# Expert attention: when a block's statistics and factors are computed

## The chip, the cores and the metric

The kernel runs on one core of a Trainium2 chip. A core has five engines that run side by side, each through its own list of instructions in order: TensorE (PE: matmuls, with weight loads shown as PEld), VectorE (DVE), ScalarE (ACT), GpSimd (POOL) and SyncE (SP, which issues most DMAs). An instruction that needs another engine's result waits for a semaphore, and everything behind it on its engine waits too. The metric is the device time of one execution in microseconds (us), lower is better. The kernel before takes 2578.53 us, the median of three runs.

## The reference

A small vision tower is computed: 128 images are cut into 64 tokens of 256 features by two convolutions, then come an attention with a ReLU in place of a product, an attention with experts, a linear attention and a feed-forward layer with experts. The change lies in the third, the expert attention:

```python
def _L0_ffn_ref(x, norm_w, router_w, router_b, qkv_w, proj_w, proj_b, out_w):
    residual = x
    mean = jnp.mean(x, axis=-1, keepdims=True)
    var = jnp.mean((x - mean) ** 2, axis=-1, keepdims=True)
    xn = (x - mean) / jnp.sqrt(var + EPS) * norm_w
    gate = jax.nn.softmax(xn @ router_w.T + router_b, axis=-1)
    ...
    attn = jnp.einsum('bcehtd,bcehsd->bcehts', q, k) * scale
    attn = jax.nn.softmax(attn, axis=-1)
    y = jnp.einsum('bcehts,bcehsd->bcehtd', attn, v)
    ...
    out = jnp.einsum('btceo,bte->btco', y, gate).reshape(B, T, D)
    return residual + out @ out_w.T
...
h = h + _L0_ffn_ref(_layernorm(h, axis=-1), L0_ffn_norm_w, ...)
```

Each token is normalised twice in a row: ahead of this layer (`_layernorm`), where the result is also the layer's residual, and inside it. Both follow from the mean and the variance of the token's 256 features, by a few factors for each token: `rs` and `mr` for the stream (`h` plus its normalised form), `ra` for the layer's input.

## The kernel before

The stream lies in SBUF as `h2`, 128 partitions x 64 pairs x 256 features: a pair is two images, whose 2 x 64 tokens fill the partitions. The expert attention goes through the pairs in the loop of `rest` (L1349), one pair in each turn. In a turn it computes the scores of the current pair (L1116), takes their maxima and subtracts them on VectorE (L1126, L1130), exponentiates on ScalarE (L1133), sums on VectorE (L1136, L1137), and multiplies by the gate and the reciprocal on GpSimd (L1143, L1144). The weights of the pair before are transposed on TensorE (L1152), copied by ScalarE (L1157) and multiplied with the values (`mixed`, L1167); the pair before that gets its output product (L1183) and is added to the stream by VectorE (`added`, L1187). For the next pair, queries and keys (L1034) and values (L1057) are computed; VectorE and ScalarE copy the values out of PSUM (L1071, L1073) and GpSimd adds a bias (L1077).

Nearly all of these PSUM tiles (queries, values, transposes, outputs) come from one ring of four buffers (`sh.psq`), so a product waits until the tile four places earlier has been emptied.

Four pairs make a block. What a block needs ahead of its pairs is spread over earlier turns by a table: `at(n, place, f, ...)` files a step under a turn and a place, and the loop calls `do((p, place))` at nine places. The places that matter here are "POOL", after GpSimd's second weights and before the values, and "DVE", at the end of the turn. The steps of a block b, whose first pair is n = 4b:

- `statistics(n0)` (L863) on VectorE, for two tiles: L870 (`bn_stats`) and L871 (`bn_aggr`), the second of which writes the tile `mv` with mean and variance. Two calls make a block. For b > 2 they are filed in turns n - 11 and n - 10.
- `factors(parts)` (L882) on GpSimd, nine small instructions over 128 x 4 elements. Part 0 is L887 and L888 (a power), part 1 L891 to L893, part 2 L895 (a power) and L896, part 3 L898 and L899. For b > 2 parts 0 and 1 are filed in turn n - 9, parts 2 and 3 in turn n - 8.
- `normal(k)` (L911) on GpSimd, one tile in each of the turns n - 8 to n - 5: L915 computes the normalised tile and reads `mv` and `ra`, then `stream` (L923) updates the stream with `rs` and `mr`.
- transposes, gate logits and the gate itself in turns n - 4 to n - 1.

For the blocks from 3 on, `mv` comes from a ring of two buffers, as `rs` and `mr` do:

```python
elif n0 == 0:
    self.mv = sh.np_.tile([P, 8, 2], F32, tag="mv", name="mv")
```

The order of the instructions on each engine is the order in which the program issues them (`manual_schedule`). Steps filed under the same turn and place run in the order in which they were filed, a lower block's first.

Of the kernel before, what the change touches and what calls it, by code (L numbers as in the profile page):

```python
# [761 lines left out]
def expert_attention(c, sh, front, hd, normw, wr, br, wqkv, wvT, wproj, bproj, wout):  # L762
# [446 lines left out]
    def at(n, place, f, *a):  # L1209
        key = (n, place) if n >= 0 else "first"  # L1210
        work.setdefault(key, []).append(lambda: f(*a))

    for b, x in enumerate(blocks):
        n = NB * b
        if b > 2:
            at(n - 11, "DVE", x.statistics, 0)
            at(n - 10, "DVE", x.statistics, 2)
        if b > 1:
            if b == 2:
                at(n - 7, "POOL", x.factors)  # L1220
            else:
                at(n - 9, "POOL", x.factors, (0, 1))
                at(n - 8, "POOL", x.factors, (2, 3))
            for k in range(NB):
                at((1, 2, 2, 3)[k] if b == 2 else n - 8 + k, "POOL", x.normal, k)
        elif b == 1:
            for k in range(NB):
                at(1 + k // 2, "ACT2", x.stream_scalar, k)
        if b:
            for fc in range(2):  # L1230
                at(n - 4 + fc, "PE", x.transpose, fc)
                at(n - 4 + fc, "ACT", x.transposed, fc)
            at(n - 2, "PE", x.logits_in_strips)
            at(n - 2, "ACT", x.logits_copied)
            at(n - 1, "PE", x.logits_transposed)
            at(n - 1, "DVE0", x.logits_less_max)
            at(n - 1, "ACT1", x.exponents)
            at(n - 1, "DVE1", x.sums)
            at(n - 1, "POOL0", x.gates)
# [18 lines left out]
    x, y, z = blocks[:3]  # L1258
# [1056 lines left out]
@with_exitstack  # L2315
def vit_tower(ctx: ExitStack, tc: tile.TileContext, a, out):
    const = ctx.enter_context(tc.tile_pool(name="const", bufs=1))
    dram = ctx.enter_context(tc.tile_pool(name="dram", bufs=1, space=DRAM))
    c = Ctx(tc, const)

    hd = dram.tile([B, T, D], F32, name="hd")

    hx = dram.tile([B, T, D], F32, name="hx")
    gfd = dram.tile([B * T, 1], F32, name="gfd")
    with tc.tile_pool(name="stream", bufs=1) as sp:
        c.h2 = sp.tile([P, B // 2, D], F32, name="h2")
        tokenizer(c, a["x"], a["w1"], a["bn1"], a["w2"], a["bn2"])
        front = Front(c, hd, *(a[k] for k in ("wqk1", "bqk1", "wv1", "bv1", "wg")))
        with ExitStack() as rings:
            sh = Shared(c, rings, ExitStack())  # L2330
            beside, rest = expert_attention(
                c, sh, front, hd, *(a[k] for k in ("normw", "wr", "br", "wqkvf", "wvf", "wproj", "bproj", "wout"))
            )
            rest(*relu_attention(c, sh, a["wqkv0"], a["wmlp"], a["bmlp"], beside))
    c.tables(ctx.enter_context(tc.tile_pool(name="tables", bufs=1)))
    with tc.tile_pool(name="gate", bufs=1) as gp:
        k = Routing(c, gp, a["wg"], a["bg"])
        with front.ctx:
            linear_attention(c, front, hd, hx, out, k)
        experts(c, hx, gfd, out, a["we1"], a["we2"], a["be2"], lambda: route(c, k, gfd))  # L2340
# [71 lines left out]
```

## Time and profile before

| what | value |
|---|---|
| median of three runs | 2578.53 us (2573.55 to 2582.93) |
| profiled execution | 2578.67 us |
| its span in the profile | 2577.0 us |
| granted TensorE clock, mean | 0.987 |
| tokenizer and the ReLU attention, then the first turn of the pairs | 0 to 1101 us |
| loop over pairs, from pair 1 (1101 to 1780 us) | PE 665.1, DVE 604.9, ACT 495.4, POOL 526.8 us busy of 679 |
| linear attention and experts (1780 to 2577 us) | PE 732.2, DVE 440.5, ACT 288.9, POOL 298.3 us busy of 797 |
| L870, 64 instructions | 407 ns median |
| L871, 64 instructions | 182 ns median |

A row of the page or of an answer is read so: times are microseconds from the start of the span; an instruction is named by its engine, its line in the kernel, its operation and the tiles that it writes and reads (`out<-in`). In a timeline the first number is the start, the second the duration. `[0.16 <-PE sc L1116]` behind a row means that the engine stood idle for 0.16 us before it, and that L1116 on PE ended the wait. In a table of windows the busy time of each engine in each stretch is given, with the number of instructions in brackets.

### The profile page before, as it was taken

The page shows a single profiled execution, that of the slowest core. Times are in us where ns is not written, and L with a number is a line of the kernel's source. Part 1 is how long each engine was busy: PE and PEld are TensorE (multiplying, and loading weights), DVE is VectorE, ACT ScalarE, POOL GpSimd, SP SyncE. Part 2 cuts the span into 40 slices and gives each one's busy share as a digit, 9 for nine tenths or more (in the row PEclk, how much of TensorE's full clock was granted, in tenths as well). Part 3 has the DMA queues.
Part 4 walks back from the last instruction along what each step waited for, and adds up shares of the span by engine and source line. Part 5 has one row for each costly group of instructions (what it writes and reads, how often), then busy time and mean ns, then how long its engine had stood idle before and what let it go on. Part 6 is the DMA issues. An engine that isn't in the chain of part 4 may idle for free. (4 is left out here: it accounts for less than half of the span.)

```text
span 2577.0 us, 78108 instructions
## 1 busy us (share of the span) xinstructions
PE 2463.2 (96%) x33713; PEld 1623.6 (63%) x33713; DVE 2011.8 (78%) x3000; ACT 1631.8 (63%) x3421; POOL 1701.0 (66%) x1491
## 2 busy tenths in 40 slices
PE   7989999999999999899999999999999968999997
PEld 4554444444444444477777777776566547888886
DVE  5759999999999989898898889887667794444443
ACT  2228889898988888776777777775544433323332
POOL 3418989898998999787878787864232404445453
PEclk9999999999999999999999999999999989999998
DMA  3100000000000000000000000001354335555554
GB/s 113 36 13 1 2 2 2 1 2 2 2 2 2 2 2 13 2 28 14 24 14 24 14 24 14 24 14 34 84 121 110 83 89 195 181 192 191 198 190 129
DMA packets 138033, 140.97 MB, mean 55 GB/s; under 512 B 108001, under 2 KB 121859, under 8 KB 129870
## 3 DMA queue, kind: packets, MB, share of 16 engines
q1 hardware_dynamic: 128684, 119.48, 15.5%
q0 software_dynamic: 7648, 14.77, 1.8%
q8 instruction: 267, 4.37, 0.7%
q10 hardware_dynamic: 1344, 1.61, 0.2%
q14 instruction: 90, 0.74, 0.1%
HBM read 104.00 MB, written 32.54 MB: 53 GB/s over the span
## 5 line engine op out<-in xcount | busy, mean ns | idle before, releaser
L540 POOL TENSOR_TENSOR m<-q,k 128x1024 f32<-128x1024 f32 x384 | 719.6, 1908 | 55.8 <-PE sc L342 46.8
L532 DVE TENSOR_TENSOR m<-pc,k 128x2048 f32<-128x2048 f32 (+1 forms) x320 | 646.5, 2056 | 0.5 <-ACT q L472 0.5
L342 PE MATMUL sc<-m,wide 128*32 128x512 f32 x4096 | 520.1, 597 | 8.9 <-ACT m L541 6.6
L541 ACT ACTIVATE m<-m 128x1024 f32<-128x1024 f32 x384 | 402.4, 1049 | 20.5 <-POOL m L540 20.5
L342 PEld LDWEIGHTS sc<-m,wide 128*32 128x32 f32 x4096 | 134.7, 109 | 269.4 <-issue 157.7
L550 ACT ACTIVATE m<-k,q 128x64 f32<-128x64 f32 x1024 | 270.7, 338 | 0.9 <-DVE k L419 0.9
L1144 POOL TENSOR_TENSOR e<-e,mx 128x1024 f32<-128x1024 f32 x127 | 241.6, 1902 | 9.9
L2238 PE MATMUL ph<-xt,w1s 128*128 128x256 f32 x896 | 199.0, 380 | 4.4 <-ACT hT L2242 2.2
L1157 ACT COPY pT<-pt 128x512 f32<-128x512 f32 x256 | 133.4, 597 | 109.5 <-PE pt L1152 109.5
L2254 PE MATMUL po<-w2s,hT 128*128 128x256 f32 x896 | 198.0, 379 | 0.0
L2238 PEld LDWEIGHTS ph<-xt,w1s 128*128 128x128 f32 x896 | 169.8, 190 | 29.2 <-ACT hT L2242 3.4
L2254 PEld LDWEIGHTS po<-w2s,hT 128*128 128x128 f32 x896 | 168.1, 190 | 21.7
L2272 POOL DMA_INDIRECT out<-y,rout x56 | 56.6, 1010 | 168.2 <-ACT hT L2242 129.2
L1126 DVE TENSOR_REDUCE mx<-sc 128x16 f32<-128x1024 f32 x128 | 150.3, 1215 | 21.2 <-PE sc L1116 21.2
L1136 DVE TENSOR_REDUCE mx<-e 128x16 f32<-128x1024 f32 x128 | 154.7, 1209 | 6.6 <-ACT e L1133 4.9
L1133 ACT ACTIVATE e<-e 128x1024 f32<-128x1024 f32 x128 | 133.9, 1060 | 34.3 <-DVE e L1130 30.0
L2242 ACT ACTIVATE hT<-ph,w1s 128x256 f32<-128x256 f32 x224 | 93.0, 470 | 96.9 <-PE ph L2238 82.5
L2259 ACT ACTIVATE y<-y,gf 128x256 f32<-128x256 f32 x56 | 28.0, 507 | 197.3 <-issue 112.3
L1130 DVE TENSOR_TENSOR e<-sc,mx 128x1024 f32<-128x1024 f32 x128 | 150.2, 1214 | 0.1
L1041 ACT COPY kr<-pqk 128x512 f32<-128x512 f32 x248 | 127.3, 601 | 24.2 <-PE pqk L1034 24.2
L1152 PE MATMUL pt<-ident,e 128*128 128x128 f32 x1024 | 130.5, 277 | 11.0 <-POOL e L1144 9.7
L1167 PEld LDWEIGHTS pz<-pT,vr 128*64 128x64 f32 x4096 | 124.7, 138 | 21.1 <-issue 10.6
(346 smaller groups left out, 4856.5 us busy)
## 6 DMA issues: line engine op xcount, KB each, us to landing
w1s<-in_we SPq DMA_DIRECT2D x30, 1028.0 KB
w2s<-in_we SPq DMA_DIRECT2D x30, 1024.0 KB
h<-hd SPq DMA_DIRECT2D x4, 2048.0 KB
hx<-h SPq DMA_DIRECT2D x4, 2048.0 KB
out<-h SPq DMA_DIRECT2D x4, 2048.0 KB
xt<-in_x SPq DMA_DIRECT2D x15, 512.0 KB
hd<-h SPq DMA_DIRECT2D x15, 512.0 KB
x<-hd SPq DMA_DIRECT2D x12, 512.0 KB
```

The costliest lines, as they stand in the source:

```text
L342: nc.tensor.matmul(dst[j : j + 32], wide[:, hf, s : s + 32], part, start=start, stop=stop)
L532: nc.vector.tensor_tensor(m, bcast(self.pq[:, hf, i : i + n], 3, T), k, ALU.max)
L540: nc.gpsimd.tensor_tensor(m, bcast(self.q[:, hf, s : s + 2], 3, T), k, ALU.subtract)
L541: nc.scalar.activation(m, m, AF.Relu)
L550: nc.scalar.activation(self.parts[i, hf][:, q], self.blk.k[:, hf, i], AF.Relu, bias=self.q[:, hf, i - NB // 2, q : q + 1], scale=-1.0,)
L1126: nc.vector.tensor_reduce(mx, self.sc[x].rearrange("p h c s -> p (h c) s"), AX.X, ALU.max)
L1130: nc.vector.tensor_sub(e, self.sc[x].rearrange("p h c s -> p (h c) s"), bcast(self.sm[x], 2, T))
L1133: nc.scalar.activation(self.e[x], self.e[x], AF.Exp, scale=SCALE)
L1136: nc.vector.tensor_reduce(self.sm[x], self.e[x], AX.X, ALU.add)
L1144: eng.tensor_mul(e, e, bcast(sm, 2, T))
L2238: nc.tensor.matmul(ph[:, j], self.w1[:, w0 : w0 + P], self.xt[:, fc], start=(fc == 0), stop=(fc == 1))
L2254: nc.tensor.matmul(po, self.hT[:, f, r * P : r * P + P], self.w2[:, f, :], start=(f == 0), stop=(f == 7))
```

## The change

For the blocks from 4 on, `early` is 2. Their statistics are filed two turns sooner, in turns n - 13 and n - 12. Their factors are filed one part a turn, in turns n - 11, n - 10, n - 9 and n - 8, so that the last part stays where it was and the first moves up by two turns. Blocks 0 to 3 are as before. No instruction is added or removed.

```diff
     for b, x in enumerate(blocks):
         n = NB * b
+        early = 2 * (b > 3)
         if b > 2:
-            at(n - 11, "DVE", x.statistics, 0)
-            at(n - 10, "DVE", x.statistics, 2)
+            at(n - 11 - early, "DVE", x.statistics, 0)
+            at(n - 10 - early, "DVE", x.statistics, 2)
         if b > 1:
             if b == 2:
                 at(n - 7, "POOL", x.factors)
+            elif early:
+                for k in range(4):
+                    at(n - 11 + k, "POOL", x.factors, (k,))
             else:
                 at(n - 9, "POOL", x.factors, (0, 1))
                 at(n - 8, "POOL", x.factors, (2, 3))
```

## The prediction

> **What bounds the kernel now.** I read the page's busy shares first, then the loop over pairs as one window for each pair, then the timeline of one pair boundary, then who waits for whom on single lines.
>
> ```profile
> PE 2463.2 (96%) x33713; PEld 1623.6 (63%) x33713; DVE 2011.8 (78%) x3000; ACT 1631.8 (63%) x3421; POOL 1701.0 (66%) x1491
> ```
>
> TensorE is busiest overall, but a share says nothing about one loop. The changed code runs in the loop over pairs, and that loop repeats every four pairs. A pair is counted here from the start of its scores (L1116): pair 39 starts at 1513.11, pair 43 at 1556.07. The windows below give pairs 39 to 42 and then pairs 56 to 59 (columns: length, then busy us of PE, PEld, DVE, ACT, POOL):
>
> ```profile
> 1513.11:1523.93 10.82, 10.78 (x282) 8.51 (x278) 9.73 (x19) 7.70 (x15) 6.80 (x7) 1.00 0.01 3
> 1523.93:1535.03 11.10, 10.59 (x284) 8.54 (x281) 9.86 (x14) 7.99 (x14) 10.53 (x14) 1.00 0.01 3
> 1535.03:1545.38 10.35, 10.35 (x284) 8.57 (x280) 9.13 (x12) 8.14 (x15) 9.61 (x14) 1.00 0.14 41
> 1545.38:1556.07 10.69, 10.69 (x297) 8.54 (x293) 10.04 (x16) 7.73 (x15) 8.06 (x8) 1.00 0.12 30
> ...
> 1695.62:1706.72 11.10, 10.59 (x284) 8.54 (x281) 9.85 (x14) 7.99 (x14) 9.53 (x10) 1.00 0.02 4
> 1706.72:1717.07 10.35, 10.35 (x285) 8.57 (x281) 9.13 (x12) 8.13 (x15) 4.89 (x6) 1.00 0.14 46
> 1717.07:1727.76 10.69, 10.69 (x297) 8.54 (x293) 9.13 (x12) 7.73 (x15) 5.76 (x6) 1.00 0.09 23
> 1727.76:1738.42 10.66, 10.66 (x282) 8.51 (x279) 8.82 (x15) 7.78 (x15) 4.20 (x5) 1.00 0.01 4
> ```
>
> The second group is a free experiment: no statistics and no factors are left there (and from pair 57 no normalising), and GpSimd is nearly idle. Yet a pair costs the same, and pair 56 the same 11.10 as pair 40, which has factors ahead of it. GpSimd's load does not set the pace. Four pairs cost 42.96 with this work (39 to 42). Without it they cost 11.10 + 10.35 + 10.69 + 10.66 = 42.80, and the gain is in the last one (10.66 for 10.82).
>
> What does set it shows at the boundary from pair 39 to pair 40:
>
> ```profile
> 1522.50 0.36 DVE L1187 TENSOR_TENSOR h<-h,po 128x256 f32<-128x256 f32 x1
> 1522.66 0.21 POOL L1143 TENSOR_TENSOR mx<-mx,gate 128x16 f32<-128x16 f32 x1 [1.11 <-DVE mx L1137]
> 1523.93 1.59 PE L1116 MATMUL sc<-kr 32*64 32x64 f32 x128
> 1524.19 1.22 DVE L1071 TENSOR_TENSOR vr<-pv,xTr 128x512 f32<-128x512 f32 x2
> 1525.57 2.35 DVE L1126 TENSOR_REDUCE mx<-sc 128x16 f32<-128x1024 f32 x2 [0.16 <-PE sc L1116]
> 1526.99 1.23 POOL L915 TENSOR_SCALAR oTr<-h,mv,rs 128x256 f32<-128x256 f32 x1
> 1527.06 1.09 PE L1152 MATMUL pt<-ident,e 128*128 128x128 f32 x8 [0.51 <-POOL e L1144]
> ```
>
> In the pair whose number leaves 3 when divided by four, VectorE is late by the gate's small steps. TensorE waits for it twice: before the second values product (L1057, whose PSUM buffer L1187 empties; the line's own view names L1187 as its releaser 13 times, 6.2 us, once in four pairs) and before the second half of the transposes (L1152, 0.51). So VectorE has little to give from L1126 of one pair to L1187 of the same pair.
>
> **The new wait.** The tile `mv` has two buffers. Statistics of block b write the buffer that block b-2 had, and its last reader is L915, the normalising of that block's fourth tile on GpSimd, in pair 4b-13. Before, statistics began in pair 4b-11, two pairs later, and nothing had to be waited for. Now they begin in pair 4b-13 itself, at the end of VectorE's queue for that pair. The first L871 of each block b = 5 to 15 must wait for that L915: 11 waits. Block 4 moves too, but the last reader of its buffer lies before this loop. Behind L871 stand the next pair's maxima (L1126), for which ScalarE's exponents, GpSimd's weights and then TensorE's transposes wait.
>
> **Its price in one boundary** (block 13, pair 39). L1071 ends at 1524.19 + 1.22 = 1525.41; L870 takes 0.42 more, to 1525.83. L915 ends at 1526.99 + 1.23 = 1528.22. VectorE stands for 2.39. Then the rest of the statistics, read from where they now lie, after pair 41:
>
> ```profile
> 1546.56 0.18 DVE L871 BATCH_NORM_AGGREGATE mv<-st 128x2 f32<-128x6 f32 x1
> 1546.66 0.40 DVE L870 BATCH_NORM_STATS2 st<-h 128x6 f32<-128x256 f32 x1
> 1547.09 0.18 DVE L871 BATCH_NORM_AGGREGATE mv<-st 128x2 f32<-128x6 f32 x1
> 1547.19 1.20 DVE L1126 TENSOR_REDUCE mx<-sc 128x16 f32<-128x1024 f32 x1
> ```
>
> From the first L871 to the maxima is 0.63, so pair 40's maxima start at 1528.85 in place of 1525.57: 3.28 late. How much of that reaches TensorE, step by step:
>
> 1. Pair 41's own chain, which waits for nothing between, takes 6.46 from maxima (1536.66) to the end of L1187 (1542.76 + 0.36). So L1187 of pair 40 ends at 1535.31. Pair 39 shows 1.07 from L1187's end (1522.86) to the next scores (1523.93): scores of pair 41 at 1536.38, not 1535.03. That is 1.35; the other 1.7 was slack.
> 2. GpSimd's weights: 6.26 from maxima to the first L1143 (1542.92 in pair 41) and 4.36 on to the end of the second L1144 (1545.37 + 1.91). For pair 40 that ends at 1539.47. TensorE reaches the second half of the transposes 2.60 after the scores (1.52 and 1.08), at 1538.98, and waits 0.49. TensorE is 1.84 late.
> 3. VectorE ends pair 40 with L1071 (7.79 after the maxima, 1.22 long) and the second half of the statistics (0.99 to the next maxima): pair 41's maxima at 1538.85, 2.19 late. Pair 41's L1187 ended about 1.2 ahead of need, so nothing is added, and no statistics follow it any more: pair 42's maxima are set by the scores again.
> 4. In pair 43 the maxima came 1.82 after the scores, because statistics stood before them; where nothing does it is 1.63 or 1.64. That returns 0.19: VectorE is 1.65 late, and pair 43 is the pair in which it decides.
>
> So four pairs cost 1.65 more. Eleven times: 18.2. After the last block the statistics of pairs 49 and 50 are gone: less 0.2. Sum +18.
>
> **The moved factors.** The nine small steps of a block stay nine. Part 0 (0.20 + 1.03 in the trace, about 1.4 with its gaps) goes behind pair 4b-11, part 1 (three of 0.20, about 0.85) behind 4b-10, part 2 (1.02 + 0.20) behind 4b-9 and part 3 (two of 0.20) ahead of the normalising. I cost them at nothing: GpSimd's idle time ahead of L1143 covers them (2.37 in pair 42, 1.11 and more in pair 43). Taking 2.1 us from behind pair 39 would let pair 40's L1143 start right after its reciprocal, but that now comes about 3 late. Without that cover part 0 would cost at most its 1.4 us. Block 4's statistics go into pair 3 without a wait; by the rows between 0 and 0.9, taken as 0. No DMA is issued by a moved step and SP's order stays.
>
> Bounds for four pairs: at the top the whole 3.28 (11 x 3.28 = 36); at the bottom step 1 alone less step 4, 1.16 (13). A gain is bounded by pairs 56 to 59: 0.16 in four pairs, 2 in all.
>
> The Trainium skill, Perfetto Trace Analysis, section Optimization Strategy, says that the same gap repeating over a stretch can mean that there are too few buffers for the next tile. By that reading the moved statistics make such a gap, a bubble of full size every four pairs, and the sum would be the 36 of the upper bound; the rows above let 1.63 of each 3.28 be absorbed. The same page, section GPSIMD Engine Instruction, distrusts GpSimd's reported spans and advises start-to-start spacing, which for L915 is 1.33 here (1526.99 to 1528.32) instead of 1.23: about 1 us more in all.
>
> **The rivals.**
> - *All of it arrives* (slower still). Later waits of the ring of four PSUM buffers could pass on what step 1 calls slack: 2578.7 + 36 = 2615. Against it: L1187 ends 1.7 ahead of need in pair 40.
> - *VectorE's idle time swallows it* (not slower). It is busy 38.8 of 42.96, so 4.2 is free against a stall of 2.4. It decides if L1187 of pair 40 may come 3.07 later without anyone waiting. The trace speaks against: 1535.03 - 1.07 leaves 1.72. Time 2577 to 2580.
> - *GpSimd's lateness in pair 40 was on the path* (faster). L1143 starts 0.9 after its reciprocal there (1532.85, against 1531.71 + 0.25). If that 0.9 reached TensorE and the new wait did not: 11 x 0.9 = 10, 2569. Pair 56 speaks against it: no factors ahead, and the same 11.10.
> - *The change doesn't act as read*: no wait, because the second buffer is free in time. L915 would have to end before 1525.83; it ends 2.39 later, by two weights of 1.90 that go before it. Then 2577 to 2580, counted with the second rival.
>
> **How the numbers follow.** The profiled execution took 2578.67: its span of 2577.0 and 1.67 around it. The median of the three runs is 2578.53, so both bases agree. Forecast: 2577.0 + 18 + 1.67 = 2597. Chances: forecast 0.80 (its own range, from the bottom of 13 to some 29: 2591 to 2608), all of it 0.12, swallowed or not acting 0.06, faster 0.02. For 8 in 10 the range reaches down for a part of the swallowed case and up to the bound: 2588 to 2614. What a measurement can tell from no change is 0.3%, 7.7 us: slower means above 2586. Slower 0.92, same 0.06, faster 0.02.
>
> **What would show it.** After: VectorE idle before L871, released by GpSimd's L915, 11 times and about 2.4 each, 26 in all; four pairs take 44.6; L1057's wait for L1187 doubles in count; the maxima of the pair after each wait come some 5 after their scores instead of 1.64; times from pair 52 on shift only. The prediction is wrong if L871 has no GpSimd wait, if the four pairs stay at 43.0, or if the pairs without a wait grow too.

## The result

The changed kernel takes 2600.59 us (median of six runs, 2599.38 to 2605.42), the kernel before in the same comparison 2578.32 (2573.55 to 2583.15). The ratio is 1.0088 with a 95% interval from 1.0071 to 1.0104: slower by 0.9%, some 22 us. The prediction said 2597, with a range from 2588 to 2614.

The profiled execution after has a span of 2597.7, 20.7 more than before. Its busy times hardly differ from before, which is the first thing to read in it: no engine got more work.

```profile
PE 2471.4 (95%) x33713; PEld 1625.6 (63%) x33713; DVE 2008.5 (77%) x3000; ACT 1632.6 (63%) x3421; POOL 1701.6 (66%) x1491
```

The same four pairs as before, 39 to 42, as one window each (length, then busy us of PE, PEld, DVE, ACT, POOL):

```profile
1528.46:1539.12 10.66, 10.66 (x282) 8.51 (x279) 8.82 (x15) 7.78 (x15) 7.22 (x10) 1.00 0.01 3
1539.12:1551.58 12.46, 11.01 (x284) 8.66 (x281) 9.80 (x16) 7.21 (x13) 9.06 (x10) 1.00 0.01 3
1551.58:1562.65 11.07, 10.85 (x283) 8.70 (x281) 10.73 (x18) 8.92 (x16) 9.32 (x11) 1.00 0.13 38
1562.65:1573.34 10.69, 10.69 (x297) 8.54 (x293) 9.13 (x12) 7.73 (x15) 9.46 (x10) 1.00 0.13 31
```

The pair after the wait went from 11.10 to 12.46, the next from 10.35 to 11.07, the pair of the wait itself from 10.82 to 10.66. Four pairs take 44.88 in place of 42.96: 1.92 more. The eleven blocks with the wait make 11 x 1.92 = 21.1. From the scores of pair 4 to those of pair 63 the trace has 658.40 against 636.85, 21.55 more, so the loop holds all of the loss. The pairs from 52 on, behind the last wait, have their old lengths.

VectorE at the boundary from pair 39 to pair 40, with GpSimd's L915, in the timeline after:

```profile
1540.51 0.42 DVE L870 BATCH_NORM_STATS2 st<-h 128x6 f32<-128x256 f32 x1
...
1542.17 1.23 POOL L915 TENSOR_SCALAR oTr<-h,mv,rs 128x256 f32<-128x256 f32 x1
...
1543.44 0.18 DVE L871 BATCH_NORM_AGGREGATE mv<-st 128x2 f32<-128x6 f32 x1 [2.51 <-POOL oTr L915]
...
1544.07 2.32 DVE L1126 TENSOR_REDUCE mx<-sc 128x16 f32<-128x1024 f32 x2
...
1546.31 2.35 DVE L1130 TENSOR_TENSOR e<-sc,mx 128x1024 f32<-128x1024 f32 x2
...
1547.58 2.22 PE L1034 MATMUL pqk<-xTr 64*64 64x256 f32 x32 [0.91 <-DVE e L1130]
```

L870 was done at 1540.93. L871 stood for 2.51 until L915 was done with `mv`, and the maxima came 4.95 after their scores (1539.12), where before it was 1.64. The last row is the one that the prediction did not have: TensorE's queries and keys (L1034) now wait for VectorE's L1130. L1034's own view, taken from 1190 us on, shows it in ten of the eleven waits (microseconds in total, times; one row of PE and two of PEld for each wait, so the sum counts some time twice). In the kernel before, the same view lists no wait at all:

```profile
  DVE e L1130: 24.3, 30
```

L871's own view over the whole span names L915 eleven times, by the three tiles that it writes in turn; before, it lists no wait:

```profile
  POOL xTr L915: 10.1, 4
  POOL xnr L915: 10.1, 4
  POOL oTr L915: 7.5, 3
```

### The profile page after: what moved, and what is told of

It reads as the page before. It is cut to its first block, busy times and chain, and to the rows that moved or that the text cites. A ratio compares the mean times of both kernels' runs of the same rounds, so it can differ in the third digit from the quotient of the medians.

```text
span 2597.7 us, 78064 instructions
## 1 busy us (share of the span) xinstructions
PE 2471.4 (95%) x33713; PEld 1625.6 (63%) x33713; DVE 2008.5 (77%) x3000; ACT 1632.6 (63%) x3421; POOL 1701.6 (66%) x1491
## 5 line engine op out<-in xcount | busy, mean ns | idle before, releaser
L1144 POOL TENSOR_TENSOR e<-e,mx 128x1024 f32<-128x1024 f32 x127 | 241.6, 1902 | 9.9
L1130 DVE TENSOR_TENSOR e<-sc,mx 128x1024 f32<-128x1024 f32 x128 | 150.1, 1213 | 0.1
L1152 PE MATMUL pt<-ident,e 128*128 128x128 f32 x1024 | 132.4, 278 | 11.2 <-POOL e L1144 8.9
L1041 ACT COPY kr<-pqk 128x512 f32<-128x512 f32 x248 | 127.3, 601 | 17.4 <-PE pqk L1034 17.3
L1167 PEld LDWEIGHTS pz<-pT,vr 128*64 128x64 f32 x4096 | 124.7, 138 | 21.1 <-issue 13.6
```

Of the source, the lines that this page charges most:

```text
L1130: nc.vector.tensor_sub(e, self.sc[x].rearrange("p h c s -> p (h c) s"), bcast(self.sm[x], 2, T))
L1144: eng.tensor_mul(e, e, bcast(sm, 2, T))
```

## The experiments

Every run is compared with the kernel before on the same chip. Its median there was 2580.81 for the first four experiments, and 2580.43 for the last four, which ran on another chip.

**Three buffers for `mv`.** If the loss is the wait, a third buffer ends it, and the statistics stay where the change put them. The tile was also cut from eight columns to the four that are used.

```diff
-                self.mv = sh.np_.tile([P, 8, 2], F32, tag="mv", name="mv")
+                self.mv = sh.np_.tile([P, NB, 2], F32, tag="mv3", name="mv", bufs=3)
```

> The changed kernel with three buffers for mv in blocks 3 to 15 (and only as many columns as are used), so the buffer that block b writes was last read four pairs earlier. Theory (the cost is the wait of L871 for L915): no idle time before L871, the pair after it falls from 12.46 to about 11.1, four pairs take 42.8 to 43.0 and the run 2576 to 2580. Rival (the cost is the place: 1.16 us of statistics put into the pair in which VectorE is late, and in the next): four pairs stay above 43.5 and the run above 2586.

2577.91, ratio to the kernel before 0.9989 (0.9979 to 0.9999). The boundary from pair 39 to pair 40 on VectorE:

```profile
1524.55 0.41 DVE L870 BATCH_NORM_STATS2 st<-h 128x6 f32<-128x256 f32 x1
1525.00 0.18 DVE L871 BATCH_NORM_AGGREGATE mv<-st 128x2 f32<-128x6 f32 x1
1525.10 0.39 DVE L870 BATCH_NORM_STATS2 st<-h 128x6 f32<-128x256 f32 x1
1525.53 0.18 DVE L871 BATCH_NORM_AGGREGATE mv<-st 128x2 f32<-128x6 f32 x1
1525.63 2.33 DVE L1126 TENSOR_REDUCE mx<-sc 128x16 f32<-128x1024 f32 x2
```

No idle time stands before L871. The pair's length is 11.10 again and four pairs take 42.80, which is what the kernel before needs where it has no statistics at all. So the whole loss is the wait, and the new place of the statistics costs nothing in itself, though the maxima still come 2.47 after the scores (1523.16) and not 1.64: that much lateness is absorbed.

**The statistics alone.** The factors go back to their two turns.

```diff
-            elif early:
-                for k in range(4):
-                    at(n - 11 + k, "POOL", x.factors, (k,))
```

> The changed kernel with the statistics two turns early but the factors where they were, parts 0 and 1 in turn n - 9, parts 2 and 3 in turn n - 8. Theory (the statistics alone cost): the same 11 waits of 2.5 us and the same time as the changed kernel, 2597 to 2603. Rival (spreading the factors costs, or pays back part of the wait): 2590 or less if it costs 10 us or more, 2608 or more if it pays 8.

2600.83, ratio 1.0084 (1.0065 to 1.0104). The pairs have the lengths of the changed kernel (12.46, 11.07, 10.68, 10.66), and the eleven waits come to 27.7 in both. Spreading the factors neither costs nor pays, so it also returned nothing of the loss.

**A later reader.** Part 2 of the factors goes ahead of the normalising, which makes L915 end later.

```diff
-                    at(n - 11 + k, "POOL", x.factors, (k,))
+                    at(n - 11 + k, "POOLa" if k == 2 else "POOL", x.factors, (k,))
...
+                do((p, "POOLa"))
                 do((p, "POOL"))
```

> The changed kernel with part 2 of the factors ahead of that turn's normalising on GpSimd, so that L915 ends 1.3 us later and nothing else moves. Theory (the slack of the path is used up, so a longer wait reaches the end whole): the wait grows from 2.5 to 3.8 and four pairs by 1.3, 11 x 1.3 = 14, to about 2615. Rival (the four pairs are set elsewhere and the wait is a symptom, or more slack is left): below 2605.

2615.54, ratio 1.0149 (1.0122 to 1.0176). The wait and the pair that has it:

```profile
1555.72 0.18 DVE L871 BATCH_NORM_AGGREGATE mv<-st 128x2 f32<-128x6 f32 x1 [3.77 <-POOL oTr L915]
```

```profile
1550.14:1563.86 13.72, 11.21 (x284) 8.64 (x281) 9.79 (x16) 7.31 (x13) 9.07 (x10) 1.00 0.01 2
```

The wait grew by 1.26 (3.77 for 2.51) and the pair by 1.26 (13.72 for 12.46). Past the slack every microsecond of the wait arrives.

The edit moved more than was expected: L915 also makes one of the tiles that TensorE transposes next (L938), and TensorE now waits for it too. The pair's length is still set by L1130, for which L1034 waits 0.90 behind that, against 0.91 in the changed kernel:

```profile
1555.74 0.33 PE L938 MATMUL ptx<-ident,oTr 128*128 128x128 f32 x1 [1.05 <-POOL oTr L915]
1559.86 2.23 PE L1034 MATMUL pqk<-xTr 64*64 64x256 f32 x32 [0.90 <-DVE e L1130]
```

**The addition first.** This tells step 1 of the prediction (L1187 comes late and holds the values, L1057) from the link that the profile after shows (L1130 holds L1034).

```diff
                 do((p, "ACT1"))
+                if older:
+                    older.added()
                 do((p, "DVE1"))
...
                 cur.weights(0)
-                if older:
-                    older.added()
                 old.mixed_copied()
```

> The changed kernel with the addition to the stream (L1187) put ahead of the gate's and the weights' sums on VectorE, so that it ends 1.5 us or more earlier in each pair and sums start 0.3 later. Step 1 of the prediction (L1187 late, so the values product L1057 late): the pair after the wait falls from 12.46 to about 11.1, the run to about 2585. Other theory, from the profile after (the queries' and keys' product L1034 waits for L1130, which empties the scores' PSUM buffer): that pair stays at 12.3 to 12.5, only the 0.34 that the pair before it waits for L1187 goes, and the run takes 2595 to 2600.

2600.46, ratio 1.0077 (1.0055 to 1.01): far from the 2585 of step 1, and 0.5 above the range of the second theory. L1057's view from 1190 us on has no wait for L1187 left, and L1034 waits for L1130 as before the edit (24.4, 30 times). The two pairs:

```profile
1528.71:1538.85 10.14, 10.14 (x283) 8.36 (x279) 8.63 (x15) 7.64 (x15) 6.88 (x10) 1.00 0.02 3
1538.85:1551.83 12.98, 10.95 (x285) 8.43 (x281) 10.01 (x17) 7.35 (x14) 9.41 (x10) 1.00 0.01 3
```

Pair 39 lost its wait (10.66 to 10.14) and pair 40 grew by the same 0.52, because the wait of L871 ends when L915 does and not sooner. The second theory had missed this: it gave pair 40 at most 12.5, and it took 12.98. But with L1187 early, pair 40 did not fall to 11.1. Step 1 named the wrong link.

The three kernels with late maxima and the one with three buffers give the slack of the link that does hold. Lateness is the time from scores to maxima less the 1.64 of before, and pair 40 is compared with the 11.10 of before in every row:

| kernel | maxima late by | pair 40 longer by | absorbed |
|---|---|---|---|
| three buffers | 0.83 | 0.00 | all |
| the change | 3.31 | 1.36 | 1.95 |
| addition first | 3.83 | 1.88 | 1.95 |
| later reader | 4.57 | 2.62 | 1.95 |

**One turn early.** The kernel before with the statistics in turns n - 12 and n - 11, two buffers. The program has the same eleven waits of L871 for GpSimd, but the L915 that they wait for lies one pair back.

```diff
-            at(n - 11, "DVE", x.statistics, 0)
-            at(n - 10, "DVE", x.statistics, 2)
+            at(n - 11 - (b > 3), "DVE", x.statistics, 0)
+            at(n - 10 - (b > 3), "DVE", x.statistics, 2)
```

> The kernel before with the statistics of blocks 4 to 15 one turn early in place of two (turns n - 12 and n - 11), two buffers, factors where they were. The program carries the same 11 waits of L871 for L915, but L915 then lies a turn back. Theory (only what the wait ends on counts): no idle time before L871, and as the statistics leave the pair before the one in which VectorE is late, four pairs take 42.8 in place of 42.96: 2575 to 2579. Rival (statistics at the end of a pair of the first and second kind cost, or a wait in the program costs by itself): 2585 or more.

2577.98, ratio 0.9993 (0.9983 to 1.0003). L871's own view lists the 11 wait instructions, 21 ns each, and no idle time for GpSimd:

```profile
L871 DVEq EVENT_SEMAPHORE  x11: 21/21/21, 1192.0 to 1622.3; - x11
```

The pairs are 11.11, 10.35, 10.68, 10.66, so four take 42.80. Here the eleven waits in the program cost nothing, since L915 was done when VectorE got to them.

**The gate's sums last.** By the prediction's reading VectorE's chain in the fourth pair sets the pace, and in the profile before a gap of 0.78 stands in that chain, ahead of L986:

```profile
1520.81 0.17 DVE L986 TENSOR_REDUCE gm<-gate 128x4 f32<-128x16 f32 x1 [0.78 <-ACT gate L983]
```

Two kernels take the gate's sums, and GpSimd's product behind them (L990), to the end of the turn, one with three buffers and one from the kernel before:

```diff
-            at(n - 1, "DVE1", x.sums)
-            at(n - 1, "POOL0", x.gates)
+            at(n - 1, "DVE", x.sums)
+            at(n - 1, "DVE", x.gates)
```

> Three buffers for mv, and the gate's sums, reciprocal and product (L986, L987, L990) moved from ahead of the weights' sums to the end of the turn, so that VectorE no longer waits 0.78 for ScalarE's gate exponents ahead of L1136 in each fourth pair. Theory (VectorE's chain in that pair sets the pace): L1187 and the weights come 1.1 earlier there, both of TensorE's waits go (0.5 for L1187, 0.51 for L1144), four pairs take 41.8 in place of 42.8, 15 times: 2560 to 2567. Rival (the pace is TensorE's own work): 2574 to 2579.

> The kernel before with only the gate's sums, reciprocal and product moved to the end of the turn. Theory as for the three buffers: about 1.0 less in four pairs; the statistics still cost 0.16 there or are hidden now: 2561 to 2569. Rival (the pace is TensorE's own work): 2576 to 2581.

With three buffers 2565.46, ratio 0.9942 (0.9928 to 0.9957); in the kernel before 2568.27, ratio 0.9961 (0.9946 to 0.9975). Both are faster than the kernel before and than the changed one. Pairs 39 to 42 with three buffers:

```profile
1502.95:1513.09 10.14, 10.14 (x282) 8.36 (x279) 9.08 (x15) 7.64 (x15) 7.62 (x9) 1.00 0.01 3
1513.09:1523.57 10.48, 10.48 (x284) 8.54 (x280) 10.26 (x18) 8.11 (x15) 9.42 (x11) 1.00 0.01 3
1523.57:1533.92 10.35, 10.35 (x284) 8.57 (x280) 10.04 (x16) 8.14 (x15) 8.49 (x11) 1.00 0.13 39
1533.92:1544.61 10.69, 10.69 (x296) 8.54 (x293) 9.12 (x12) 7.74 (x15) 9.50 (x11) 1.00 0.13 32
```

In each row PE's busy time now equals the length. The four pairs take 41.66, and in them both of TensorE's waits are gone, the one for L1187 and the one for L1144. The edit takes 1.14 off four pairs with three buffers (from 42.80) and 1.00 in the kernel before (42.96 to 41.96).

**Three buffers and the addition first.** The changed kernel with the edits of the first and the fourth experiment together.

> Three buffers for mv, and L1187 ahead of the gate's and the weights' sums as in the fourth run. Theory (with the stall gone nothing sets L871's end, but the weights still come when they did): the pair that waited for L1187 falls from 10.66 to 10.14 and the next grows by as much, because its transposes wait for the same L1144: 2576 to 2580. Rival (the 0.5 is kept): 15 x 0.5 less, 2569 to 2572.

2575.20, ratio 0.9978 (0.9966 to 0.9989), 0.8 under the range of the theory. By the pairs the theory holds: the one that waited for L1187 falls to 10.14 and the next grows to 11.63 (from 11.10), and the transposes there wait 1.04 for the weights, where they waited 0.51:

```profile
1523.19 1.09 PE L1152 MATMUL pt<-ident,e 128*128 128x128 f32 x8 [1.04 <-POOL e L1144]
```

Curing one of two waits that end on the same chain moved it to the other.

## Why the prediction was right

**What bounds the loop.** Right. VectorE's chain in the fourth pair sets the pace: taking the gate's steps out of it shortened four pairs by 1.14. Making VectorE later in the pair behind it cost in full once the slack was used up.

**The wait and its size.** Right. Eleven waits of L871 for L915, 2.5 each (27.7 in all, where the prediction had 26), and only these: three buffers bring the time back. The predicted 2.39 was short by 0.12: L870 starts 0.08 before L1071's reported end (1540.51, against 1539.37 + 1.22), and L871 begins 0.04 after L915's.

**Step 1, how the lateness reaches TensorE.** The size was right, 1.36 against 1.35, and the link was wrong, so this part of the number is luck. "L1187 ends at 1535.31 ... scores of pair 41 at 1536.38" led over the ring of four PSUM buffers. What holds TensorE is the other PSUM ring: `all_queries_keys` writes two tiles into the two buffers of the scores (L1026), and L1130 empties these. The description of the kernel before puts the queries into the ring of four; in this loop they are not there. The addition-first kernel took the predicted link away, and the pair stayed long. The rows of pair 40 before already held the real link:

```profile
1527.84 2.34 DVE L1130 TENSOR_TENSOR e<-sc,mx 128x1024 f32<-128x1024 f32 x2
...
1531.41 1.96 PE L1034 MATMUL pqk<-xTr 64*64 64x256 f32 x32
```

L1130 was done with both tiles at 1530.18, 1.23 ahead of L1034. With maxima 3.31 later it could not stay ahead. After, L1034 starts when the first tile is free, waits again in its middle for the second, and takes 2.22 in place of 1.96. Counted from the maxima's lateness, the predicted link absorbs 1.93 (3.28 less 1.35) and the real one 1.95. That the two lie so close is chance, and it is why the number came out. The sign that should have shown the predicted link, L1057 waiting for L1187 twice as often, did not appear: 12 waits and 4.1 us, against 13 and 6.2.

**Step 2, the weights late for the transposes.** Too small in sum: 0.49 predicted, and the pair grew by 0.72 (11.07 for 10.35). Rows of the profile after show where:

```profile
1552.06 1.39 PEld L1116 LDWEIGHTS sc<-kr 32*64 32x64 f32 x120 [0.28 <-ACT kr L1041]
...
1553.52 2.27 PE L1152 MATMUL pt<-ident,e 128*128 128x128 f32 x16
...
1554.69 0.86 PEld L1152 LDWEIGHTS pt<-ident,e 128*128 128x128 f32 x8 [0.31 <-POOL e L1144]
```

The transposes (L1152) take 2.27 in place of 1.97, so the predicted wait for the weights is there, with some 0.30. The other 0.42 lies ahead of them: L1116 of pair 41 takes 2.02 in place of 1.59, since ScalarE's copies of the late queries and keys (L1041) reach it late. This is a consequence of the link that step 1 missed. The 0.23 by which step 2 was too small makes most of the difference between +18 and +21.

**Steps 3 and 4.** Right: pair 42 is unchanged (10.69), and the fourth pair gives back 0.16 (10.66 for 10.82), predicted 0.19.

**The factors at nothing.** Right, by the run with the statistics alone.

**The rivals.** Not all of the lateness arrived (1.92 of 3.31). VectorE's idle time did not swallow it, though 4.2 was free in four pairs: it lies in other places than the wait. GpSimd's lateness in pair 40 was not on the path: with three buffers L1143 starts 0.08 after its reciprocal there (1531.86, against 1531.53 + 0.25), where it was 0.89 before, and the pair takes 11.10 as before. And the change acts as read, since the eleven waits are there.

The Trainium skill, Perfetto Trace Analysis, section Optimization Strategy, says that a gap repeating on the engine that should be saturated can mean too few buffers. That holds here as to cause, though the gap stands on VectorE and only part of it reaches TensorE, the busiest engine: 27.7 us of such gaps went with a third buffer. The page names no price. The 36 of the prediction was its own reading of the page as a gap of full size, and the trace differs from it, since 1.95 of each delay was absorbed. The same page, section GPSIMD Engine Instruction, advises to time GpSimd by start-to-start spacing and not by the reported span. For the end of this wait the reported span came nearer: L915 started at 1542.17 and took 1.23 by its row, and L871 began at 1543.44, 1.27 after that start, not the 1.34 to the next start (1543.51).

**The sum.** +18 predicted; the span grew by 20.7 and the median by 22.3.

## What to carry to other kernels

Before a step is moved up, ask who last reads the buffer that it will write, and where that reader stands in its own queue: with two buffers one turn up was free here, and two turns up cost 0.9%. What a wait cost here was the lateness of the work queued behind it (3.31), less the slack of the first engine that needed that work (1.95), and then 0.72 more in the pair behind it. That slack has to be looked for on every ring of buffers that the late engine empties, not only on the one whose wait the profile shows today. One chain fed two waits here: removing one of them moved its time to the other, and shortening the chain removed both in the four pairs read.

## What was not expected

Single pairs are longer by up to 1.4 in one execution and not in the next, and some of them are often the same pair: pair 34 takes 11.74 in the kernel before, 11.73 after, 12.01 with the statistics one turn early, but 10.68, the usual length, with three buffers and the addition first; pair 25 took 12.45 after and 10.74 before. In pair 25 after, TensorE stands 1.42 in the middle of the scores (L1116), and in pair 34 before 0.89 in the middle of the transposes (L1152). The weight loads there wait for nothing that the profile shows, so the cause stays open. From pair 8 to pair 51 such pairs add 2.2 us in the profile before and some 2.8 after, which is why the readings above go by the lengths that repeat.
